# Layer 3 of five images: y not stored and loaded back, but convolved again from the residual in the closing loop

## The chip, the core and the metric

One core of one Trainium2 chip runs the whole program. The metric is the device time of one execution in microseconds (us). The kernel before takes 2627.5 us, the median of 3 runs (2625.96 to 2628.13).

The engines are named as in the profile: PE is TensorE (matrix products), DVE is VectorE, ACT is ScalarE, POOL is GpSimd, and SP is SyncE, which here only issues transfers (DMAs). Each engine works through its own queue in order.

## The reference, cut to what matters

The input `x` is 16 images of 64 channels by 128 by 128, fp32. Four layers follow each other, each a residual branch on a group-normalised input:

```python
x = x + _L0_conv_ref(_gn(x), L0_conv_conv_w)
x = x + _L1_conv_ref(_gn(x))
x = x + _L2_conv_ref(_gn(x), L2_conv_W, L2_conv_b)
x = x + _L3_conv_ref(_gn(x), L3_conv_w_bin, ...)
```

Layer 3 is the one that the change touches:

```python
y = _conv(x, w_bin, [(1, 1), (1, 1)])
y = _conv(y, w1x1, [(0, 0), (0, 0)]) + b1x1[None, :, None, None]
mean = jnp.mean(y, axis=(0, 2, 3), keepdims=True)
var = jnp.var(y, axis=(0, 2, 3), keepdims=True)
y = (y - mean) * jax.lax.rsqrt(var + EPS)
...
y = jnp.where(y >= 0, y, LEAK * y)
return jnp.clip(y, 0.0, CEIL)
```

Its mean and variance run over all 16 images. So no output of layer 3 can be finished before the last image has been convolved. Clipping at 0 makes the leaky branch vanish: the result is min(relu(y * scale + shift), 255), added to the residual.

## The kernel before

The image is cut by rows. A half image has 64 rows; a chunk is 8 rows of both halves, so an image has 8 chunks (`NS`), and a tile of one chunk has 128 partitions (64 channels, two halves) by 1024 elements, 512 KB. Three stages, `Front` (layers 0 and 1), `Layer2` and `Layer3`, run as a software pipeline: in each step, each stage does one chunk, of different images, in four quarters (`q` = 0 to 3). The order of the instructions on every engine is the order in which the Python code issues them (`InOrder`, line 63, keeps it); one helper on line 73 issues everything, which is why the profile puts nearly every instruction down to L73. The stages pass images through DRAM: `x2_d` after layer 1, `x3_d` after layer 2 (the residual that layer 3 adds to) and `y_d` after layer 3's convolution.

Layer 3's two convolutions are folded into one 3x3 convolution with 64x64 weights per tap (`w3`, line 209, filled by `weights_of_layer_3`). `Layer3.at` makes y of a chunk from differences and sums of rows, adds up its mean and its squares (`bn_sum`, `bn_sq`), and one step later stores it to `y_d` with four DMAs (from line 1040), each of 64 partitions with rows of 512 bytes.

After the last chunk the closing part begins. `parts` (line 1095) lists 128 pieces, 8 for each image; a piece is a tile of 128 partitions with 4 KB of an image in each (`whole`, line 1098: two partitions to a channel). For each piece, `fetch` (line 1113) takes two free tiles from `room` and loads y and the residual into them. `room` is filled, from 8 steps before the last image's first chunk of layer 3 was due, with the buffers that earlier stages no longer need, 38 tiles in all; one piece is fetched in every step from there on (line 1175), then as many as there is room for. From line 1187 the sums become a scale `sc` and a shift `sh`. Then the closing loop (line 1212) runs over all pieces: one ACT Relu over y, one DVE operation that takes the minimum with 255 and adds the residual, one store of 512 KB to `out`, and a new fetch when more than 8 tiles are free.

Products of two fp32 operands appear as two records each on PE. Products that use only 64 rows and 64 columns of the array can run four abreast, one in each quarter; `section` issues layer 2's and layer 3's remaining products in that way.

Of the kernel before, what the change touches and what calls it, by code (L numbers as in the profile page):

```python
# [10 lines left out]
F32 = mybir.dt.float32  # L11
AF = mybir.ActivationFunctionType
ALU = mybir.AluOpType
AX = mybir.AxisListType

B, C, H, W = 16, 64, 128, 128
P = 128
HW = H * W
HH = H // 2
NP = H // 2  # L20
R = 8
NS = HH // R
EARLY = 3
CP = 4
GN_EPS = 1e-5
BN_EPS = 1e-5
# [14 lines left out]
TO_PAIRS = [(0, 0, 0, 1), (0, 0, 1, 0), (0, 1, 0, 0), (1, 0, 1, 2), (1, 1, 0, 2), (1, 1, 1, 1)]  # L41
# [68 lines left out]
def tile_kernel(ctx: ExitStack, tc: tile.TileContext, x, cw_h, w2_t, b2, wbin_t, w1_t, b1, gamma, beta, consts, out):  # L110
    nc = tc.nc
    pe, dve, act, sp, pool = (InOrder(tc, e) for e in (nc.tensor, nc.vector, nc.scalar, nc.sync, nc.gpsimd))
    PSUM = bass.MemoryType.PSUM

    cpool = ctx.enter_context(tc.tile_pool(name="cpool", bufs=1))
# [5 lines left out]
    def k(name):  # L121
        return kc[:, AT[name][0]:AT[name][1]]

    def const(shape, name):
        return cpool.tile(shape, F32, name=name)

    cwh = const([P, C], "cwh")
    b2_sb, b1_sb, gamma_sb, beta_sb = (const([P, 1], n) for n in ("b2_sb", "b1_sb", "gamma_sb", "beta_sb"))
    bn_sum = cpool.tile([P, B * NS], F32, name="bn_sum")
    bn_sq = cpool.tile([P, B * NS], F32, name="bn_sq")  # L130

# [2 lines left out]
    x3_d = [dram.tile([C * HW], F32, name=f"x3_d{b}") for b in range(B)]  # L134
# [21 lines left out]
    ring = ctx.enter_context(tc.tile_pool(name="ring", bufs=2))  # L156
    stp = ctx.enter_context(tc.tile_pool(name="stp", bufs=2))
    ps_two = ctx.enter_context(tc.tile_pool(name="ps_two", bufs=2, space=PSUM))
    ps_one = ctx.enter_context(tc.tile_pool(name="ps_one", bufs=1, space=PSUM))
    ps_po = ctx.enter_context(tc.tile_pool(name="ps_po", bufs=1, space=PSUM))  # L160
# [289 lines left out]
    rows = []  # L450
# [363 lines left out]
    class Layer2:  # L814
# [55 lines left out]
        def done(self, co):  # L870

            edge = {}
            for half in ("lower", "upper"):
                edge[half] = sv(f"edge_{half}", 2)
                pool.tensor_scalar_mul(edge[half], co[:, 0:2], k(half))
            coefs3[self.b] = co, edge

        def square(self, i):
            act.activation(
# [99 lines left out]
    class Layer3:  # L979
# [34 lines left out]
        def at(self, i, q):  # L1014
            b = self.b
            n = b * NS + i
            if q == 0 and 0 <= i < NS:
                t = self.v[i]
                one = ps_one.tile([P, CP, W], F32, tag="one", name=f"one3_{b}_{i}")
                two = ps_two.tile([P, 2, CP, W], F32, tag="two", name=f"two3_{b}_{i}")  # L1020
                self.p[i] = two, one
                shared(one, w3[:, 2], t)
                if not both_layers(now[0]):
                    own(two[:, 0], 0, TO_PAIRS, w3, d3, packed["pk3"], d2[0])
            if q == 1:
                if 0 <= i < NS:
                    two, one = self.p[i]
                    if both_layers(now[0]):
                        for k in range(2):
                            own(two[:, k], k, TO_PAIRS, w3, d3, None)  # L1030
                        apart(two, TO_PAIRS, w3, d3)
                    else:
                        own(two[:, 1], 1, TO_PAIRS, w3, d3, packed["pk3"], d2[0])
                    self.v.pop(i)
                    self.c = ring.tile([P, CP * W], F32, tag="c3", name=f"c3_{b}_{i}", bufs=1)
                    act.activation(self.c, flat(one), AF.Identity, bias=b1_sb)
                if i + 1 < NS:
                    self.prepare(i + 1)
                if 1 <= i:
                    y = self.y.pop(i - 1)  # L1040
                    for s in range(2):
                        for z in range(2):
                            v = pairs(y_d[b], s)[:, (i - 1) * R:i * R, :].rearrange("c (n z) w -> c z n w", z=2)
                            sp.dma_start(v[:, z], y[s * C:(s + 1) * C, z])
            if q == 2:
                alone = not both_layers(now[0] + 1)
                if i + 1 < NS and alone:
                    even, odd, _ = self.v[i + 1]
                    difference(d3, spread(even, W), odd)
# [12 lines left out]
            if q == 3:  # L1062
                if i + 1 < NS and not both_layers(now[0] + 1):
                    self.twin()
                if 0 <= i < NS:
                    act.activation(
                        junk, self.y[i].rearrange("p s j w -> p (s j w)"), AF.Square,
                        accum_out=bn_sq[:, n:n + 1],
                    )
# [22 lines left out]


    N = R * W
    parts = [(b, q) for b in range(B) for q in range(C * HW // P // N)]
    room, loaded = deque(), deque()

    def whole(d, q):
        return d.rearrange("(p n) -> p n", p=P)[:, q * N:(q + 1) * N]

    def rest(pool, tag, shape, bufs, n=None):
        for m in range(bufs if n is None else n):
            t = pool.tile([P] + shape, F32, tag=tag, name=f"end_{tag}_{len(room)}", bufs=bufs)
            while len(t.shape) > 2:
                t = t.rearrange("p a b c -> p (a b) c" if len(t.shape) == 4 else "p a b -> p (a b)")
            room.append(t[:, 0:N])
# [5 lines left out]

    def fetch():
        n = fetched[0]
        if n < len(parts):
            b, q = parts[n]
            yt, rt = room.popleft(), room.popleft()
            sp.dma_start(yt, whole(y_d[b], q))
            sp.dma_start(rt, whole(x3_d[b], q))
            loaded.append((yt, rt))  # L1120
            fetched[0] += 1

    for step in range(starts[2][1] - 2, steps):
        now[0] = step
        for q in range(4):
# [46 lines left out]
                n = 3 if step == last_one else 1 if step < last_one + NS - 2 else 0  # L1172
                rest(ring, "x3", [2, CP, W], NS + 2, n)

            if step >= last_one - NS and q == 3 and len(room) > 1:
                fetch()
    while chains:
        tick()
    rest(ring, "x3", [2, CP, W], NS + 2, NS + 2 - 3 - (NS - 3))
    rest(ring, "y", [2, CP, W], 2)  # L1180
    rest(ring, "v3", [R + 2, W], 2)
    while len(room) > 1:
        fetch()

    mv = cpool.tile([P, 2], F32, name="mv")
    dve.tensor_reduce(mv[:, 0:1], bn_sum, axis=AX.X, op=ALU.add)
    dve.tensor_reduce(mv[:, 1:2], bn_sq, axis=AX.X, op=ALU.add)

    pm = sm(2)
    pe.matmul(pm, k("bnavg"), mv, start=True, stop=True)
    me = cpool.tile([P, 2], F32, name="me_bn")
    dve.tensor_copy(me, pm)
    var = cpool.tile([P, 1], F32, name="var_bn")
    dve.scalar_tensor_tensor(var, me[:, 0:1], me[:, 0:1], me[:, 1:2], op0=ALU.mult, op1=ALU.subtract)
    dve.tensor_scalar(var, var, -1.0, BN_EPS, op0=ALU.mult, op1=ALU.add)
    sd = cpool.tile([P, 1], F32, name="sd_bn")
    act.activation(sd, var, AF.Sqrt)
    r0 = cpool.tile([P, 1], F32, name="r0_bn")  # L1200
    dve.reciprocal(r0, sd)
    e = cpool.tile([P, 1], F32, name="e_bn")
    dve.scalar_tensor_tensor(e, var, r0, r0, op0=ALU.mult, op1=ALU.mult)
    dve.tensor_scalar(e, e, -0.5, 1.5, op0=ALU.mult, op1=ALU.add)
    sc = cpool.tile([P, 1], F32, name="sc")
    dve.tensor_mul(sc, r0, e)
    dve.tensor_mul(sc, sc, gamma_sb)
    sh = cpool.tile([P, 1], F32, name="sh")
    dve.tensor_mul(sh, me[:, 0:1], sc)
    dve.tensor_sub(sh, beta_sb, sh)  # L1210

    for b, q in parts:
        yt, rt = loaded.popleft()
        act.activation(yt, yt, AF.Relu, bias=sh, scale=sc)
        dve.scalar_tensor_tensor(rt, yt, 255.0, rt, op0=ALU.min, op1=ALU.add)
        sp.dma_start(whole(out[b].rearrange("c h w -> (c h w)"), q), rt)
        room.extend((yt, rt))

        if len(room) > 8:
            fetch()  # L1220


# [36 lines left out]
```

## Time and profile before

| what | value |
|---|---|
| median of 3 runs | 2627.5 us |
| the profiled execution, its own time | 2633.98 us |
| its span, first to last instruction | 2632.2 us |
| PE busy | 2068.1 us, 79% of the span, 15748 records |
| DVE busy | 2085.6 us, 79% |
| ACT busy | 1988.8 us, 76% |
| POOL busy | 410.9 us, 16% |
| DMA, read from and written to DRAM | 346.23 MB and 268.44 MB |
| granted PE clock, mean | 0.892 |

How to read it. The page gives busy time of each engine, then the span in 40 equal slices of 65.8 us: each digit is an engine's busy share of that slice in tenths (9 is 90% or more), and two rows below give the mean busy share of the core's 16 DMA engines and what they moved. A second part is the chain of waits: followed back from the last instruction, at each step to what released it. A third lists groups of equal instructions by engine, operation, output and input tile: count, busy time in us, mean of one in ns, then the idle time before them and what ended it. The table of stretches gives the same busy times for chosen windows, with the granted PE clock, the DMA share and GB/s. In SP's rows an `SPq` entry is the issue of a DMA; the transfer itself lands later. Tile names come from the program; `end_...` are the free tiles of the closing part, and `xw`, `xh`, `d2b` and `q` are older buffers used as such.

### The profile page before, as it was taken

Reading aid. Unit: us, or ns where it says so; the run is one execution under the profiler, and the core shown is the slowest. Engines: PE = TensorE matmul, PEld = TensorE weight load, DVE = VectorE, ACT = ScalarE, POOL = GpSimd, SP = SyncE. Lnnn points to the kernel's source line nnn. Section 1 sums busy time; section 2 is a strip of 40 time slices with the busy share of each in tenths; the row PEclk is TensorE's granted clock in tenths of the full one; section 3 lists DMA queues with packets and bytes.
Section 4 is the critical chain, followed back from the end, with each engine's and each line's share of the span. In section 5 each row is a group of like instructions: output and inputs, shape, how many; then the busy total and the mean of one; then the engine's idle time right before and its main releaser. Section 6 shows DMA issues by size and latency. Waiting matters only on the chain.

```text
span 2632.2 us, 45566 instructions
## 1 busy us (share of the span) xinstructions
PE 2068.1 (79%) x15748; PEld 822.4 (31%) x15748; DVE 2085.6 (79%) x2759; ACT 1988.8 (76%) x3297; POOL 410.9 (16%) x623
## 2 busy tenths in 40 slices
PE   6578899999999999999999999999999990000000
PEld 4333433434343434333333433333333330000000
DVE  4998989999999999999999999999994335333332
ACT  4778889898989898989989888888986575333332
POOL 3332322112111112121212122111101000000000
PEclk8689999999999999999999999999999995555555
DMA  8789979898888888888989877787867779999999
GB/s 206 203 230 240 238 187 240 210 235 217 231 227 222 224 221 228 216 225 219 245 210 250 201 192 202 191 209 201 211 173 184 201 211 372 419 419 419 419 419 376
DMA packets 682261, 654.48 MB, mean 249 GB/s; under 512 B 56320, under 2 KB 576672, under 8 KB 682032
## 3 DMA queue, kind: packets, MB, share of 16 engines
q1 hardware_dynamic: 668208, 613.83, 80.5%
q0 software_dynamic: 13824, 37.75, 5.5%
q8 instruction: 125, 2.05, 0.3%
q14 instruction: 104, 0.85, 0.1%
HBM read 346.23 MB, written 268.44 MB: 234 GB/s over the span
## 4 chain that ended last, share of the span: by engine, by line
PE 45%; DMA 23%; DVE 11%; ACT 9%; SPq 7%; issue 3%; POOL 0%; DVEq 0%; ACTq 0%; POOLq 0%
PE two L73 23%; PE one L73 15%; SPq L73 7%; DVE u L73 4%; PE bank L73 3%; PE po L73 3%; ACT v L73 2%; DVE e L73 2%; DMA v<-x_d 2%; DMA end_x<-x_d 2%; DMA out<-end_x 2%; DMA x_d<-u 2%; DMA x<-in_x 2%; DMA out<-xw 2%; DMA end_x<-y_d 2%
## 5 line engine op out<-in xcount | busy, mean ns | idle before, releaser
L73 PE MATMUL two<-d,w 64*64 64x512 f32 (+2 forms) x2992 | 692.4, 593 | 0.0
L73 PE MATMUL one<-v,w 128*64 128x508 f32 (+2 forms) x1600 | 362.5, 585 | 11.3 <-ACT c L73 10.8
L73 PE MATMUL one<-v,wi 128*64 128x508 f32 (+3 forms) x1536 | 350.9, 591 | 0.0
L73 PEld LDWEIGHTS two<-d,w 64*64 64x64 f32 (+1 forms) x2992 | 206.7, 134 | 415.1 <-issue 406.7
L73 DVE SCALAR_TENSOR_TENSOR e<-e 128x1032 f32<-128x1032 f32 (+1 forms) x256 | 313.3, 1224 | 0.0
L73 ACT ACTIVATE xh<-po,co 128x128 f32<-128x128 f32 (+1 forms) x480 | 274.4, 621 | 24.8 <-PE po L73 19.8
L73 DVE SCALAR_TENSOR_TENSOR y<-two,c 128x1024 f32<-128x1024 f32 x128 | 156.2, 1221 | 93.4 <-ACT v L73 63.4
L73 PE MATMUL po<-x,abd 64*64 64x512 f32 (+1 forms) x1024 | 189.5, 623 | 49.8 <-ACT xh L73 46.5
L73 PE MATMUL two<-q,cross 64*64 64x508 f32 (+3 forms) x944 | 216.1, 573 | 0.0
L73 ACT ACTIVATE v<-x,co 128x1024 f32<-128x1024 f32 (+3 forms) x256 | 203.8, 847 | 0.0
L73 ACT ACTIVATE v<-v,co 128x1154 f32<-128x1154 f32 x128 | 172.1, 1345 | 28.6 <-DMA v<-x_d 24.0
L73 DVE TENSOR_TENSOR d<-v 128x1024 f32<-128x1024 f32 x128 | 156.3, 1221 | 47.0 <-ACT v L73 29.2
L73 DVE SCALAR_TENSOR_TENSOR u<-xh 128x1170 f32<-128x1170 f32 x128 | 175.9, 1374 | 12.1 <-DMA x_d<-u 5.9
L73 POOL DMA_DIRECT2D q<-d2b x138 | 72.1, 526 | 721.5 <-DVE d2b L73 412.9
L73 PE MATMUL two<-d2a,wi 128*64 128x508 f32 (+1 forms) x768 | 183.2, 589 | 0.0
L73 PE MATMUL two<-d2b,wi 128*64 128x508 f32 (+3 forms) x768 | 176.6, 569 | 0.0
L73 PEld LDWEIGHTS one<-v,w 128*64 128x64 f32 x1600 | 110.3, 137 | 209.7 <-issue 162.7
L73 DVE SCALAR_TENSOR_TENSOR u<-xh,co,u 128x1024 f32<-128x1024 f32 x128 | 163.9, 1280 | 15.0 <-ACT u L73 14.9
L73 POOL DMA_DIRECT2D q<-d2a x138 | 73.8, 537 | 642.1 <-issue 276.1
L73 DVE SCALAR_TENSOR_TENSOR u<-e,co,u 128x1024 f32<-128x1024 f32 x128 | 164.2, 1283 | 8.2 <-DVE u L73 0.5
L73 DVE SCALAR_TENSOR_TENSOR x<-two,c 128x1024 f32<-128x1024 f32 x128 | 156.7, 1225 | 14.5 <-ACT junk L73 0.5
L73 ACT ACTIVATE edges<-v,co 64x8 f32<-64x8 f32 x512 | 156.3, 305 | 11.0 <-POOL co L73 0.9
(174 smaller groups left out, 3687.1 us busy)
## 6 DMA issues: line engine op xcount, KB each, us to landing
x<-in_x SPq DMA_DIRECT2D x256, 256.0 KB, 4.1
x_d<-u SPq DMA_DIRECT2D x512, 128.0 KB, 3.2
y_d<-y SPq DMA_DIRECT2D x512, 128.0 KB, 3.5
x_d<-x SPq DMA_DIRECT2D x496, 128.0 KB, 2.8
xr<-in_x SPq DMA_DIRECT2D x120, 512.0 KB, 5.8
v<-x_d SPq DMA_DIRECT2D x448, 72.1 KB, 3.0
v<-x_d SPq DMA_DIRECT2D x224, 144.2 KB, 2.9
end_x<-x_d SPq DMA_DIRECT2D x39, 512.0 KB, 10.0
```

Source lines behind the costliest of these rows:

```text
L73: return self.tc.keep_in_program_order(call(*args, **kwargs))
```

## The change

`AGAIN` names images 3 to 7. For them:

- `Layer3.at` still makes y and adds its mean and squares to the sums, but y isn't stored. The layer's norm coefficients of these images are kept (`kept`).
- In the closing part they have 40 chunks in place of 40 pieces. A list `todo` mixes the 40 chunks with the 88 pieces of the other images: two chunks, eight pieces, then chunks with one or two pieces between, and eight pieces after the last. For a chunk, `fetch` takes one tile and loads the residual alone, in the half-image layout: two DMAs of 64 partitions by 4 KB.
- A chunk goes through stages in three turns of the loop. `again_in` normalises its residual into a `v3` tile with one row above. `again_close` adds the row below, which comes from the next chunk, and `again_products` issues 36 products of 64x64 by 512 (nine taps, two groups of four rows, two halves), and two products with the identity that bring the second four rows' residual to the other half. `again_out` does a Relu and a min-and-add for each group of four rows, and stores 512 KB in four DMAs of 64 partitions by 2 KB.
- The sums are turned into two scales and shifts, one for each layout. `v3`'s two tiles leave `room`, so it has 36. In each step before the closing loop, fetching goes on until at least two tiles have been asked for.
- Ten DMAs of 32 KB bring the rows next to the middle of the five images into `w2`, which is free by then.

The diff, without the constants' layout and the small arithmetic of the scales:

```diff
+AGAIN = (3, 4, 5, 6, 7)
...
             coefs3[self.b] = co, edge
+            if self.b in AGAIN:
+                pool.tensor_copy(kept[:, AGAIN.index(self.b)], co[:, 0:2])
...
                     y = self.y.pop(i - 1)
-                    for s in range(2):
+                    for s in range(0 if b in AGAIN else 2):
...
-    parts = [(b, q) for b in range(B) for q in range(C * HW // P // N)]
-    room, loaded = deque(), deque()
+    parts = deque((b, q) for b in range(B) if b not in AGAIN for q in range(C * HW // P // N))
+    again = deque((b, i) for b in AGAIN for i in range(NS))
+    todo, ahead, behind = [], 8, 6
+    share = len(parts) - ahead - behind
+    for n in range(NS * len(AGAIN)):
+        todo.append(("again",) + again.popleft())
+        while n > 0 and len(todo) - n - 1 < ahead + (n - 1) * share // (NS * len(AGAIN) - 2):
+            todo.append(("loaded",) + parts.popleft())
+    todo += [("loaded",) + part for part in parts]
...
     def fetch():
...
+        else:
+            t = room.popleft()
+            for h in range(2):
+                sp.dma_start(t[cols(h)], halves(x3_d[b], h, q * R, R))
+            loaded.append((t,))
+        fetched[0] += 1
+        return len(loaded[-1])
+
+    def again_in(b, i, t):
...
+        v = ring.tile([P, R + 2, W], F32, tag="v3", name=f"v_again_{b}_{i}")
+        r = t.rearrange("p (j w) -> p j w", w=W)
+        if i == 0:
+            pool.memset(v[lo, 0, :], 0.0)
+            again_norm(n, v[hi, 0, :], xe[hi, n], hi)
+        else:
+            again_norm(n, v[:, 0, :], at_hand[-1][1][:, R - 1, :])
+        again_norm(n, v[:, 1:R + 1, :], r)
+        at_hand.append((v, r, b, i))
...
+            if step == last_one + NS - 1 and q == 2:
+                again_in(*todo[0][1:], loaded[0][0])
+
+            if step >= last_one - NS and q == 3:
+                n = 0
+                while n < 2 and len(room) > 1:
+                    n += fetch()
...
-    rest(ring, "v3", [R + 2, W], 2)
...
+    def again_products():
+
+        v, r, b, i = at_hand[-1]
+        two = ps_two.tile([P, 2, CP, W], F32, tag="two", name=f"two_again_{b}_{i}")
+        pool_, tag = ((ps_po, "po"), (ps_one, "one"))[(b * NS + i) % 2]
+        rest_ = pool_.tile([P, CP, W], F32, tag=tag, name=f"rest_again_{b}_{i}")
+        for h in range(2):
+            pe.matmul(rest_[cols(1 - h)], k("I")[cols(h), cols(h)], r[cols(h), CP:R, :], start=True, stop=True)
+        order = [(ky, kx) for kx in (1, 0, 2) for ky in range(3)]
+        for n, (ky, kx) in enumerate(order):
+            o0, o1 = (0, W) if kx == 1 else (1, W) if kx == 0 else (0, W - 1)
+            for g in range(2):
+                for h in range(2):
+                    j = g * CP + ky
+                    pe.matmul(
+                        two[cols(h if g == 0 else 1 - h), g, :, o0:o1], rows_of[ky, h][:, kx],
+                        v[cols(h), j:j + CP, o0 + kx - 1:o1 + kx - 1], start=n == 0, stop=n + 1 == len(order),
+                    )
+        summed.append((two, rest_, r, b, i))
+
+    def again_out():
+
+        two, rest_, r, b, i = summed.popleft()
+        to = out[b].rearrange("c h w -> (c h w)")
+        for g, (tag, add) in enumerate((("c2", r[:, 0:CP, :]), ("c3", rest_))):
+            z = ring.tile([P, CP * W], F32, tag=tag, name=f"z_{b}_{i}_{g}", bufs=1)
+            act.activation(z, flat(two[:, g]), AF.Relu, bias=shb, scale=sc[:, 1:2])
+            to_rows = flat(r[:, g * CP:(g + 1) * CP, :])
+            dve.scalar_tensor_tensor(to_rows, z, 255.0, flat(add), op0=ALU.min, op1=ALU.add)
+            for h in range(2):
+                sp.dma_start(halves(to, h if g == 0 else 1 - h, i * R + g * CP, CP), to_rows[cols(h)])
+        room.append(flat(r))
...
-    for b, q in parts:
-        yt, rt = loaded.popleft()
-        act.activation(yt, yt, AF.Relu, bias=sh, scale=sc)
-        dve.scalar_tensor_tensor(rt, yt, 255.0, rt, op0=ALU.min, op1=ALU.add)
-        sp.dma_start(whole(out[b].rearrange("c h w -> (c h w)"), q), rt)
-        room.extend((yt, rt))
-
-        if len(room) > 8:
+    for n, (way, b, q) in enumerate(todo):
+        if way == "again":
+            (t,) = loaded.popleft()
+            if n > 0:
+                again_close(t)
+                again_products()
+                coming.append((b, q, t))
+        else:
+            yt, rt = loaded.popleft()
+            act.activation(yt, yt, AF.Relu, bias=sh[:, 0:1], scale=sc[:, 0:1])
+            dve.scalar_tensor_tensor(rt, yt, 255.0, rt, op0=ALU.min, op1=ALU.add)
+            sp.dma_start(whole(out[b].rearrange("c h w -> (c h w)"), q), rt)
+            room.extend((yt, rt))
+            if len(summed) > 1 or summed and n > len(todo) - 3:
+                again_out()
+            if coming:
+                again_in(*coming.popleft())
+            elif n == len(todo) - behind + 1:
+                again_close(None)
+                again_products()
+        while len(room) > 8 and fetched[0] < len(todo):
             fetch()
+    while summed:
+        again_out()
```

More of the change, by code (lines that the diff above doesn't have):

```diff
@@ L127, in tile_kernel @@
     cwh = const([P, C], "cwh")
-    b2_sb, b1_sb, gamma_sb, beta_sb = (const([P, 1], n) for n in ("b2_sb", "b1_sb", "gamma_sb", "beta_sb"))
+    b2_sb, b1_sb = (const([P, 1], n) for n in ("b2_sb", "b1_sb"))
+    gamma_sb, beta_sb = (const([P, 2], n) for n in ("gamma_sb", "beta_sb"))
+    kept = const([P, len(AGAIN), 2], "kept")
     bn_sum = cpool.tile([P, B * NS], F32, name="bn_sum")
@@ L1094, in tile_kernel, with again_norm @@
     N = R * W
-    parts = [(b, q) for b in range(B) for q in range(C * HW // P // N)]
-    room, loaded = deque(), deque()
+    parts = deque((b, q) for b in range(B) if b not in AGAIN for q in range(C * HW // P // N))
[7 more added lines that the diff above has]
+    todo += [("loaded",) + part for part in parts]
+    room, loaded, at_hand = deque(), deque(), deque(maxlen=2)
+    def again_norm(n, dst, src, rows=slice(0, P)):
+        act.activation(dst, src, AF.Identity, bias=kept[rows, n, 1:2], scale=kept[rows, n, 0:1])
     def whole(d, q):
@@ L1114, in fetch @@
         n = fetched[0]
-        if n < len(parts):
-            b, q = parts[n]
+        if n == len(todo):
+            return 2
+        way, b, q = todo[n]
+        if way == "loaded":
             yt, rt = room.popleft(), room.popleft()
@@ L1120, in fetch @@
             loaded.append((yt, rt))
-            fetched[0] += 1
+        else:
[6 more added lines that the diff above has]
+    def again_in(b, i, t):
+        n = AGAIN.index(b)
+        v = ring.tile([P, R + 2, W], F32, tag="v3", name=f"v_again_{b}_{i}")
[7 more added lines that the diff above has]
+        at_hand.append((v, r, b, i))
     for step in range(starts[2][1] - 2, steps):
@@ L1173, in tile_kernel @@
                 rest(ring, "x3", [2, CP, W], NS + 2, n)
-            if step >= last_one - NS and q == 3 and len(room) > 1:
-                fetch()
+            if step == starts[1][1] + NS * B + 1 and q == 0:
+                xe = w2.rearrange("p a k c -> p (a k c)")[:, 0:len(AGAIN) * W].rearrange("p (b w) -> p b w", w=W)
+                for n, again_b in enumerate(AGAIN):
+                    for h, row in ((0, HH), (1, HH - 1)):
+                        sp.dma_start(
+                            xe[cols(h), n], x3_d[again_b].rearrange("(c r w) -> c r w", c=C, w=W)[:, row, :]
+                        )
[5 more added lines that the diff above has]
+                    n += fetch()
     while chains:
@@ L1180, in tile_kernel @@
     rest(ring, "y", [2, CP, W], 2)
-    rest(ring, "v3", [R + 2, W], 2)
-    while len(room) > 1:
+    while len(room) > 1 and fetched[0] < len(todo):
         fetch()
@@ L1189, in tile_kernel @@
     dve.tensor_reduce(mv[:, 1:2], bn_sq, axis=AX.X, op=ALU.add)
[L1191 to L1198, printed above, removed]
+    pm = sm(4)
@@ new lines, in tile_kernel, with pair @@
+    pe.matmul(pm[:, 0:2], k("bnavg"), mv, start=True, stop=True)
+    pe.matmul(pm[:, 2:4], k("same"), mv, start=True, stop=True)
+    me = cpool.tile([P, 2, 2], F32, name="me_bn")
+    dve.tensor_copy(me[:, 0], pm[:, 0:2])
+    dve.tensor_scalar_mul(me[:, 1], pm[:, 2:4], 1.0 / (B * HW))
+    mean, square = me[:, :, 0], me[:, :, 1]
+    def pair(name):
+        return cpool.tile([P, 2], F32, name=name)
+    var = pair("var_bn")
+    dve.tensor_mul(var, mean, mean)
+    dve.tensor_sub(var, square, var)
@@ L1199, in tile_kernel @@
+    dve.tensor_scalar_add(var, var, BN_EPS)
+    sd = pair("sd_bn")
     act.activation(sd, var, AF.Sqrt)
-    r0 = cpool.tile([P, 1], F32, name="r0_bn")
+    r0 = pair("r0_bn")
     dve.reciprocal(r0, sd)
-    e = cpool.tile([P, 1], F32, name="e_bn")
-    dve.scalar_tensor_tensor(e, var, r0, r0, op0=ALU.mult, op1=ALU.mult)
+    e = pair("e_bn")
+    dve.tensor_mul(e, var, r0)
+    dve.tensor_mul(e, e, r0)
     dve.tensor_scalar(e, e, -0.5, 1.5, op0=ALU.mult, op1=ALU.add)
-    sc = cpool.tile([P, 1], F32, name="sc")
+    sc = pair("sc")
@@ L1206, in tile_kernel @@
     dve.tensor_mul(sc, r0, e)
     dve.tensor_mul(sc, sc, gamma_sb)
-    sh = cpool.tile([P, 1], F32, name="sh")
-    dve.tensor_mul(sh, me[:, 0:1], sc)
+    sh = pair("sh")
+    dve.tensor_mul(sh, mean, sc)
     dve.tensor_sub(sh, beta_sb, sh)
-    for b, q in parts:
-        yt, rt = loaded.popleft()
-        act.activation(yt, yt, AF.Relu, bias=sh, scale=sc)
-        dve.scalar_tensor_tensor(rt, yt, 255.0, rt, op0=ALU.min, op1=ALU.add)
-        sp.dma_start(whole(out[b].rearrange("c h w -> (c h w)"), q), rt)
-        room.extend((yt, rt))
-        if len(room) > 8:
+    shb = cpool.tile([P, 1], F32, name="shb")
@@ new lines, in tile_kernel, with again_close @@
+    dve.scalar_tensor_tensor(shb, sc[:, 1:2], b1_sb, sh[:, 1:2], op0=ALU.mult, op1=ALU.add)
+    rows_of = {(kk, i): w3[cols(i), slot, :, cols(o)] for slot, i, o, kk in TO_PAIRS}
+    def again_close(r_next):
+        v, _, b, i = at_hand[-1]
+        n = AGAIN.index(b)
+        if i + 1 == NS:
+            pool.memset(v[hi, R + 1, :], 0.0)
+            again_norm(n, v[lo, R + 1, :], xe[lo, n], lo)
+        else:
+            again_norm(n, v[:, R + 1, :], r_next[:, 0:W])
+    def again_products():
[14 more added lines that the diff above has]
+                        v[cols(h), j:j + CP, o0 + kx - 1:o1 + kx - 1], start=n == 0, stop=n + 1 == len(order),
+                    )
+        summed.append((two, rest_, r, b, i))
@@ new lines, in tile_kernel @@
+    rows_of = {(kk, i): w3[cols(i), slot, :, cols(o)] for slot, i, o, kk in TO_PAIRS}
+    summed, coming = deque(), deque()
+    for n, (way, b, q) in enumerate(todo):
[5 more added lines that the diff above has]
+                coming.append((b, q, t))
+        else:
+            yt, rt = loaded.popleft()
[11 more added lines that the diff above has]
+        while len(room) > 8 and fetched[0] < len(todo):
@@ L1244 @@
         "b1": both(L3_conv_b1x1),
-        "gamma": twice(L3_conv_gamma),
-        "beta": twice(L3_conv_beta),
+        "gamma": laid(np.concatenate([twice(L3_conv_gamma), both(L3_conv_gamma)], axis=1)),
+        "beta": laid(np.concatenate([twice(L3_conv_beta), both(L3_conv_beta)], axis=1)),
         "consts": constants(),
```

## The prediction

> **What bounds the kernel now.** I read the 40 slices of the page first, because the kernel has a long first part and a short last one.
>
> ```profile
> PE   6578899999999999999999999999999990000000
> ...
> DMA  8789979898888888888989877787867779999999
> GB/s 206 203 230 240 238 187 240 210 235 217 231 227 222 224 221 228 216 225 219 245 210 250 201 192 202 191 209 201 211 173 184 201 211 372 419 419 419 419 419 376
> ```
>
> For 33 slices of 65.8 us TensorE (PE) is full; in the last seven it does nothing and the transfers run flat at 419 GB/s. So there are two bounds, one after the other: PE to about 2185 us, DMA from there to 2632.2 us. The chain of waits says the same from 2184 us on, and nothing else stands in it:
>
> ```profile
> 2184.56 3.51 DVE xw L73 x3
> 2188.08 9.34 DMA out<-xw
> 2197.48 10.29 DMA out<-end_xr
> 2207.79 10.00 DMA xh<-x_d
> 2217.86 9.95 DMA end_xr<-y_d
> ```
>
> The tail's groups and the DMA queue's own waits, both taken from 2200 to 2600 us, show who waits for whom there:
>
> ```profile
> L73 ACT ACTIVATE end_x<-end_x,sh,sc 128x1024 f32<-128x1024 f32 x34 | 41.9, 1238 | 79.5 <-DMA end_x<-y_d 79.5
> ...
> SPq L73 <- DMA out<-end_x: 30.1, 34, 0.9
> ```
>
> ScalarE (ACT) waits for loads to land, and SyncE (SP) waits for earlier transfers to land before it issues the next; a transfer takes 10.0 us from issue to landing and one ends every 1.25 us, so eight are always out. Compute in the tail is hidden as long as it keeps up on average, since loads run 15 pieces ahead of the stores. What counts in the tail is therefore the sum of DMA time.
>
> That time isn't bytes alone. The table of stretches (core-wide: length, busy time of each engine, granted clock, DMA share, GB/s) has two places where the only traffic of weight is loads of 64 partitions by 4 KB, alternating between the lower and the upper half (x_first at 9 to 14 us, x at 46 to 49 us):
>
> ```profile
> core 0: us, PE busy (x) PEld busy (x) DVE busy (x) ACT busy (x) POOL busy (x), PEclk, DMA share, GB/s
> 9.00:14.00 5.00, 3.62 (x24) 2.92 (x24) 1.10 (x2) 0.61 (x1) 4.64 (x9) 1.00 1.04 237
> 46.00:49.00 3.00, 0.00 (x0) 0.00 (x1) 2.96 (x3) 3.00 (x5) 0.00 (x0) 1.00 1.00 243
> 2300.00:2600.00 300.00, 0.00 (x0) 0.00 (x0) 96.81 (x79) 97.44 (x80) 0.00 (x0) 0.50 1.03 419
> ```
>
> Share 1.0 in all three, but 240 GB/s for 64 partitions against 419 for the tail's 128-partition tiles. This is the line the forecast hangs on.
>
> [...]
>
> **The change, part by part.**
>
> *Tail, transfers removed and added.* Price of a 128-partition tile of 512 KB: 524,288 B / 419 GB/s = 1.251 us. Before, 128 pieces move three such tiles each: 384. After, 88 pieces make 264, and 40 chunks each load 512 KB in two 64-partition DMAs and store 512 KB in four of 64 partitions by 2 KB. At the time the closing loop begins, all tiles of the room have been asked for: 38 before; 36 after (the two v3 tiles no longer belong to it), which by the order of `todo` are chunks 0 to 5 and 15 pieces, so 6 chunk loads and 30 whole tiles. Left for the tail: 346 whole tiles before; 234 whole tiles, 34 chunk loads and 40 chunk stores after. With P for 512 KB of chunk traffic, the tail changes by 74 P - 112 x 1.251 = 74 P - 140.1 us. It breaks even at P = 1.89 us, that is 277 GB/s.
>
> For loads the nearest row is the 240 GB/s above, the same shape (64 partitions, 4 KB each, halves alternating): P = 2.18 us. For stores no row shows 64 partitions by 2 KB. [...] I take 2.18 us for stores too[...]. Sum: 74 x 2.18 - 140.1 = **+21.5 us**.
>
> Could mixing heal it? A chunk's transfers stand between 128-partition ones in the same queue[...]. The x_first loads didn't show it: 237 GB/s with eight out. I keep it for the range.
>
> *PE.* A chunk has 36 products of 64x64 by 512 columns, four side by side, and two identity products: ten rounds. The price is in the timeline, where layer 2 and layer 3 products stand four abreast (each fp32 product makes two records):
>
> ```profile
> 2043.65 0.59 PE L73 MATMUL two<-d,w 64*64 64x512 f32 x2
> 2043.67 0.59 PE L73 MATMUL two<-q,pk 64*64 64x512 f32 x2
> 2044.08 0.59 PE L73 MATMUL two<-d,w 64*64 64x512 f32 x2
> 2044.10 0.59 PE L73 MATMUL two<-q,cross 64*64 64x512 f32 x2
> 2044.51 0.59 PE L73 MATMUL two<-d,w 64*64 64x512 f32 x2
> ```
>
> From 2043.65 to 2044.51 is one round of four: 0.86 us. A chunk is 8.6 us, 40 are 344 us. A turn (one chunk and 74/38 = 1.95 pieces between) costs DMA 2 x 2.18 + 1.95 x 3.75 = 11.7 us. PE at 8.6 lies inside it, with 3.1 us to spare, so it costs nothing; if the cover were gone (chunk traffic at full rate: 2.50 + 7.31 = 9.8 us a turn) it would still fit by 1.2 us.
>
> *ACT, VectorE (DVE), SP in a turn.* ACT: one 128x1024 norm 1.24 us, two rows at most 0.49 each, two 512-column Relus at 0.68 (the row c<-one), 1.95 Relus at 1.24: 6.0 us. DVE: 1.95 x 1.22 and two half-size passes, about 3.6 us. SP: 12 issues of 0.33 to 0.65 us (`out` and `y_d` rows), 4 to 7.7 us. All under 11.7; hidden by the DMA sum. The Relu of a chunk stands on ACT ahead of later pieces and waits for PE, and its stores on SP ahead of later loads; but it is issued a whole turn after its products began, 11.7 us against 8.6, so nobody waits.
>
> *First part.* 160 stores of y go (20.97 MB) out of SP's queue, about 0.65 us of issue each. In the five stretches of images 3 to 7 (711 to 1335 us) PE is busy 615.6 of 624 us, so the most to be had is 8.4 us; the waits list puts PE's idle time there on ACT and DVE, not on a DMA. I take -2 us (0 to -8).
>
> *Handing over.* The first chunk's norm, 1.24 + 0.33 us on ACT, stands before the last Square, where ACT has room:
>
> ```profile
> 2179.05 1.06 ACT L73 ACTIVATE junk<-y 128x1024 bf16<-128x1024 f32 x1 [2.88 <-DVE y L73]
> ```
>
> so it costs nothing (1.6 us if that gap weren't there). The statistics get one more product and some five small DVE operations of 0.16 us, and the first row of chunk 0 to close before the first piece: +1 us (0 to 1.5, as transfers already issued go on meanwhile). Ten small loads of 32 KB pass through SP before the last y stores: 0 (up to 3). The five small Pool copies and the memsets are off every path: 0.
>
> **Sum.** 21.5 - 2 + 1 = +20.5 us. The profiled execution has a span of 2632.2 us within 2633.98; it becomes about 2652.7. Its time is 0.25% above the median shown, 2627.5, so I add the difference to the median: **2648 us**.
>
> **Rivals.**
> 1. *Chunk traffic at full rate, both ways* (ends faster). Place: the 64-partition loads and stores of the tail. Price: 74 x 1.251 - 140.1 = -47.5 us, with the other terms 2627.5 - 48.5 = 2579 us. It decides once chunk traffic averages over 277 GB/s. For it: [...] the sum of bytes falls by 10%. Against: 237 and 243 GB/s measured for just this shape.
> 2. *Only loads are slow; stores run at full rate.* 34 x 2.18 + 40 x 1.251 - 140.1 = -16 us, so 2611 us. [...] Against: nothing shown; it is merely unmeasured.
> 3. *PE becomes the bound.* If the half clock held all through [...], a chunk would take 17.2 us: 2184 + 40 x 17.2 + 15 for the last pieces = 2887 us. [...]
>
> **Chances.** Forecast (chunk traffic at 210 to 270 GB/s): 0.60, its own range 2632 to 2668. Rival 1: 0.17. Rival 2: 0.14. Rival 3: 0.03. Between break-even and the forecast [...]: 0.06, about 2628. The range to hold the time 8 times in 10 takes in rival 2 and not rival 1: 2608 to 2672. About 0.2% (5 us) is what a measurement here can tell from no change. Faster: 0.17 + 0.14 + 0.03 = 0.34; same: 0.05; slower: 0.61.
>
> **What would show it.** Right: in the tail a DMA share of about 1.0 at some 360 GB/s instead of 419, the 64-partition transfers slower per byte than whole tiles, PE idle about a quarter of each turn, ACT still ended by loads. Wrong: GB/s near 419 all along with an earlier end (rival 1); PE busy above 9 tenths and waits of ACT on `two_again` (rival 3); a first part that ends more than 8 us earlier.

## The result, and the profile after

| | median of its runs | lowest to highest | ratio to before, 95% interval |
|---|---|---|---|
| before | 2628.49 us (22 runs) | 2622.65 to 2646.89 | |
| after | 2638.92 us (22 runs) | 2628.18 to 2648.05 | 1.0032, 1.0018 to 1.0046 |

The change made the kernel 0.32% slower, 8.4 us by the ratio, where +20.5 was forecast. The direction was right, the size less than half. Below, microseconds worked out from ratios are the ratio times 2628. Differences between two kernels are taken from their ratios, since before's median on one chip and another lay between 2626.5 and 2628.8. The profiled execution of after took 2648.05 us (span 2645.9), 0.35% above its own median; its rates are read, not its end.

The 40 slices of after, rows of TensorE, DMA share and GB/s:

```profile
PE   6578899999999999999999999999999999978783
...
DMA  8799879898977777686878878787867679999999
GB/s 206 205 228 229 235 188 239 213 239 220 232 195 182 197 186 207 171 225 166 213 202 235 206 190 203 194 210 194 214 173 189 187 218 356 362 375 346 338 350 351
```

In the last seven slices, where PE was idle before, it is now 70 to 90% busy until the last; the DMA share is still full, but 419 GB/s have become 338 to 375. The table of stretches shows the same for after's closing loop (length, then busy us and count of PE, PEld, DVE, ACT, POOL; PE clock, DMA share, GB/s):

```profile
2200.00:2300.00 100.00, 99.98 (x888) 39.26 (x882) 41.34 (x44) 63.12 (x79) 0.40 (x2) 1.00 1.01 360
2300.00:2460.00 160.00, 131.26 (x1072) 50.97 (x1076) 50.12 (x56) 79.65 (x98) 0.80 (x4) 0.98 1.01 360
```

There are two regimes: at first PE has no gap, later it is busy 82%. The rate is 360 GB/s in both. The groups from 2200 to 2600 us (busy us, mean ns, idle before and what ended it) say who waits:

```profile
L74 PE MATMUL two_again<-v_again,w 64*64 64x508 f32 (+1 forms) x2664 | 335.4, 608 | 30.9 <-ACT v_again L74 30.9
...
L74 ACT ACTIVATE z<-two_again,shb,sc 128x512 f32<-128x512 f32 x72 | 51.6, 765 | 24.2 <-PE two_again L74 24.2
L74 ACT ACTIVATE end_x<-end_x,sh,sc 128x1024 f32<-128x1024 f32 x25 | 30.9, 1236 | 39.4 <-DMA end_x<-y_d 39.3
```

ACT waits for PE (the Relu of a chunk, `z`) as well as for loads, and PE for ACT. From these lines alone, transfers and TensorE are both suspects. That is what the experiments had to separate.

Ahead of the loop no loss is seen. ACT's timeline at the handing over, after (start us, length us; in brackets idle time before and what ended it):

```profile
2172.47 0.49 ACT L74 ACTIVATE v_again<-w,kept 64x128 f32<-64x128 f32 x1
2172.97 1.24 ACT L74 ACTIVATE v_again<-xw,kept 128x1024 f32<-128x1024 f32 x1
2175.31 1.06 ACT L74 ACTIVATE junk<-y 128x1024 bf16<-128x1024 f32 x1 [1.10 <-DVE y L74]
```

The first chunk's norm stands before the last Square, and the Square still has to wait 1.10 us for DVE: the norm was hidden. The last Square begins 3.7 us earlier than before (2175.31 against 2179.05). From one trace each this can't be told from chance: in later runs with the same first part as after it begins at 2169.93 (E9), 2170.81 (E3), 2174.16 (E2) and 2174.78 us (E12).

### The profile page after: what moved, and what is told of

Same layout as the page of the kernel before. It is cut to its first block, busy times and chain, and to the rows that moved or that the text cites. A ratio compares the mean times of both kernels' runs of the same rounds, so it can differ in the third digit from the quotient of the medians.

```text
span 2645.9 us, 52043 instructions
## 1 busy us (share of the span) xinstructions
PE 2435.8 (92%) x18790; PEld 961.9 (36%) x18790; DVE 2086.8 (79%) x2803; ACT 2070.9 (78%) x3457; POOL 413.5 (16%) x638
## 4 chain that ended last, share of the span: by engine, by line
PE 43%; DMA 19%; DVE 15%; ACT 9%; SPq 8%; issue 4%; POOL 1%; DVEq 0%; ACTq 0%; POOLq 0%
PE two L74 21%; PE one L74 14%; SPq L74 8%; DVE u L74 5%; PE bank L74 3%; DVE e L74 3%; PE two_again L74 3%; ACT v L74 3%; DMA out<-end_x 2%; PE po L74 2%; DMA x_d<-u 2%; DVE d L74 2%; DMA v<-x_d 2%; DVE y L74 2%; DMA out<-end_y 1%
## 5 line engine op out<-in xcount | busy, mean ns | idle before, releaser
L74 PE MATMUL two_again<-v_again,w 64*64 64x508 f32 (+1 forms) x2880 | 365.1, 613 | 39.1 <-ACT v_again L74 39.1
L74 PEld LDWEIGHTS two_again<-v_again,w 64*64 64x64 f32 x2880 | 134.8, 137 | 242.6 <-issue 177.2
L74 PEld LDWEIGHTS one<-v,wi 128*64 128x64 f32 x1536 | 101.0, 137 | 192.7 <-issue 154.9
```

The source lines that it names most:

```text
L74: return self.tc.keep_in_program_order(call(*args, **kwargs))
```

## The experiments

**E1 to E3: a chunk's load whole, its store whole, one tap.** The theories are named in the texts of the expectations. The edits, each alone, on the changed kernel:

```diff
 E1
-            for h in range(2):
-                sp.dma_start(t[cols(h)], halves(x3_d[b], h, q * R, R))
+            sp.dma_start(t, whole(x3_d[b], q))
 E2
-            for h in range(2):
-                sp.dma_start(halves(to, h if g == 0 else 1 - h, i * R + g * CP, CP), to_rows[cols(h)])
...
+        sp.dma_start(whole(to, i), flat(r))
 E3
-        order = [(ky, kx) for kx in (1, 0, 2) for ky in range(3)]
+        order = [(1, 1)]
```

> The changed kernel, but a chunk's residual comes as one DMA of 128 partitions by 4 KB in the pieces' layout instead of two of 64 partitions; the channels then stand in another order, so the convolved values of the five images aren't the reference's. Time of the changed kernel: 2638.9 us. Theory A (the 64-partition loads are the dear part, about 2.9 us for 512 KB; stores cost near full rate): 34 x (2.9 - 1.25) = 56 us less, about 2583. Theory B (loads cost 2.18 us as in the forecast, the stores are as dear): 34 x 0.93 = 32 us less, about 2607. Theory C (the closing loop is held by the waits of ACT and PE, not by transfers): less than 10 us less, above 2629.

> The changed kernel, but a chunk is stored by one DMA of 128 partitions by 4 KB in the pieces' layout instead of four of 64 partitions by 2 KB; rows of the five images land in another order. Theory A (stores run near full rate, about 1.4 us for 512 KB): 40 x 0.15 = 6 us less, and up to 6 more from an end that no longer runs through small stores: 2627 to 2633. Theory B (the forecast's 2.18 us): 40 x 0.93 = 37 us less, about 2602. Theory C: no difference, 2635 to 2643.

> The changed kernel with one of the nine taps of the repeated convolution, so 4 of 36 products; the five images' layer 3 is left incomplete. Theory A (transfers bound the closing loop): 2633 to 2643, no difference; at most 5 us less, from the first 100 us where PE was full. Theory C (PE bounds it): PE's 344 us shrink to about 70, so 20 us less or more, below 2619.

| | median | ratio to before, 95% interval | against after |
|---|---|---|---|
| E1 load whole | 2608.1 us | 0.9922, 0.9910 to 0.9934 | -28.9 us |
| E2 store whole | 2627.26 us | 1.0003, 0.9988 to 1.0017 | -7.6 us |
| E3 one tap | 2641.18 us | 1.0062, 1.0044 to 1.0081 | +7.9 us |

The same stretch, 2200 to 2460 us, of E3. The bytes are those of after:

```profile
2200.00:2460.00 260.00, 88.85 (x300) 25.16 (x300) 87.76 (x97) 138.57 (x170) 1.19 (x6) 0.58 1.02 361
```

PE is busy a third of the time and the rate stays at 361 GB/s, and nothing was gained. So TensorE doesn't bind the changed kernel. E3 is even 7.9 us (2 to 14) slower than after; why isn't shown. The idle times of ACT before `z` were real, but they weren't what set the end. Making the load whole gave about what the forecast's price implies (0.93 us each on 34 loads is 32 us); making the store whole gave 0.19 us each, not 0.93. I concluded then that stores of 64 partitions are cheap. That conclusion fell later.

**E4: the first part alone.** The kernel before, with y of images 3 to 7 not stored; the closing loop loads y of images 8 to 12 in its place.

```diff
-                    for s in range(2):
+                    for s in range(0 if 3 <= b < 8 else 2):
...
-            sp.dma_start(yt, whole(y_d[b], q))
+            sp.dma_start(yt, whole(y_d[b + 5 if 3 <= b < 8 else b], q))
```

> The kernel before, without the stores of y for images 3 to 7; the closing loop reads another image's y in their place, so the output of the five images isn't the reference's. Transfers of the closing loop stay as they were. It shows what the first part gains when these 160 stores go. Forecast: 2 us less. By the two profiles (the sums of the statistics begin at 2179.0 before and 2175.3 after): 4 us less, about 2624.5. Rival: nothing, 2628.

Measured: 2626.61 us, ratio 0.9992 (0.9979 to 1.0005). Leaving out the 160 stores changed nothing that can be told from noise (-5.5 to +1.3 us); -2 us is in the interval, and so is 0. That fits stores hidden behind TensorE.

**E5, E6: both whole; the same with one tap.** The edits of E1 and E2 together (E5), and the same with all taps but one left out (E6).

> Both the chunk's load and its store as one 128-partition transfer of 512 KB each; everything else as in the changed kernel. The computation is changed: a chunk's load brings 128 partitions of one image's neighbouring rows in place of the same 64 channels of two row halves, and its store writes whole tiles, so the output is another's; bytes and instruction counts of the engines stay. Theory T (the transfers' shape is all that the tail loses): 74 tiles at the whole pieces' 1.251 us less 140.1 us saved = -47.5, so about 2580. Theory S (a second loss of about 15 us that doesn't come from the shape: the TensorE-bound start of the closing loop, the drain at the end): the gains of the two single runs add up, 30.8 + 11.7 = 42.5 off 2638.9, so about 2596. If the two single runs counted the same gain twice: 2605 or more.

> As the run with both transfers whole, with one of the nine taps of the second convolution of a chunk left out but one (1 of 9 computed). Theory TensorE: the closing loop's start, where chunks lie prefetched and TensorE runs without a gap, costs the 15 us: this run is at 2580 while its sibling with nine taps is at 2596. Theory drain/DMA: no difference between the two, within 3 us.

Measured: E5 2585.04 us, ratio 0.9837 (0.9813 to 0.9860); E6 2582.87 us, ratio 0.9828 (0.9805 to 0.9851). Their stretches, E5 and then E6:

```profile
2200.00:2460.00 260.00, 252.89 (x2216) 101.22 (x2210) 103.48 (x112) 159.49 (x197) 1.59 (x8) 1.00 1.03 416
```

```profile
2200.00:2460.00 260.00, 101.01 (x348) 28.36 (x340) 102.21 (x112) 159.60 (x197) 1.59 (x8) 0.62 1.03 418
```

With whole transfers the loop runs at 416 GB/s, as before the change, though PE is busy 97% of it. The shape of the chunks' transfers (their partitions, the length of their rows and the number of DMAs together) is the whole loss: 51.2 us (44 to 58) between after and E5. Theory T (2580) is nearer than S (2596), and E6 isn't faster than E5 beyond the intervals, so TensorE at the loop's start wasn't the missing 15 us. But the single gains, 28.9 + 7.6 = 36.5 us, don't add up to 51.2. This left a question: where one kind alone is made whole, less is gained.

**E9 to E13: transfers taken away.** From the changed kernel: the 40 stores of chunks are taken away, or most of the loads of chunks, or both; E11 to E13 are also without eight of nine taps.

```diff
 E9, E11, E12
-            for h in range(2):
-                sp.dma_start(halves(to, h if g == 0 else 1 - h, i * R + g * CP, CP), to_rows[cols(h)])
 E10, E11, E13
-            for h in range(2):
-                sp.dma_start(t[cols(h)], halves(x3_d[b], h, q * R, R))
+            if not again_seen(t):
+                for h in range(2):
+                    sp.dma_start(t[cols(h)], halves(x3_d[b], h, q * R, R))
 E11, E12, E13
-        order = [(ky, kx) for kx in (1, 0, 2) for ky in range(3)]
+        order = [(ky, kx) for kx in (1, 0, 2) for ky in range(3)][:1]
```

(`again_seen` is true for a buffer of the program that a load has gone to before; slices of one buffer, such as those of `xw`, count as one.)

The expectations speak of 7 loads that stay and 33 that go. The traces of E10, E11 and E13 show ten chunk loads of 256 KB, so 5 chunks are loaded and 35 aren't. In after, six chunk loads are issued before the first Relu of the closing loop (2180.15 us), and the seventh follows at 2189.2 us. So 34 loads of the closing loop are missing, as many as the prediction counted, and the prices below are worked out with 34 loads and 40 stores.

> The changed kernel without the 40 stores (512 KB each, as four 64-partition transfers) of its chunks; their part of the output is not written. What the time falls by, over 40, is a store's price. By the forecast (2.18 us each): 2638.9 - 87 = 2552. By what the two whole-store runs gave (11.7 us of shape over 40 with split loads, 20.9 with whole loads, on 1.25): 1.54 to 1.77 each, so 2568 to 2577.

> The changed kernel with only the first 7 of 40 chunk loads: the other 33 chunks are computed from what the buffer held, so their part of the output is another's. What the time falls by, over 33, is a load's price. By the forecast (2.18 us each): 2638.9 - 72 = 2567. By the whole-load runs (30.8 us of shape over 33 with split stores, 43.5 with whole stores, on 1.25): 2.18 to 2.57 each, so 2554 to 2567. TensorE can't be done before about 2535.

> Neither those 33 loads nor the 40 stores, and one tap of nine, so that only the whole pieces move in the closing loop: what they cost alone. At 1.251 us a tile: 2627.5 - 140 = 2487. If the whole pieces were slower for another reason than the chunks' traffic beside them (the order, the 8 in flight, the end), this run is above 2487 by that much: 2495 to 2503.

> No chunk stores (their output is not written) and one tap of nine: whole pieces and the split chunk loads only, TensorE out of the way. Against the run with neither (ratio 0.9471, 2489 us), the rise over 33 is a load's price. Forecast's price 2.18: 2489 + 72 = 2561. A dear load of 2.57 (from the whole-load run beside whole stores): 2574. If TensorE was no part of the matter, the time stays at the 2587 of the run with nine taps (2.98 each).

> Only the first 7 chunk loads (the other chunks are computed from what the buffer held, so their output is another's) and one tap of nine: whole pieces and the split chunk stores only. The rise over the run with neither, by 40, is a store's price. Forecast's price 2.18: 2489 + 87 = 2576, as with nine taps. A cheap store of 1.54: 2550; of 1.25 (full rate): 2539. If load and store come out together at 147 us, nothing arises from their mixture; if at much less, the mixture costs the rest.

| what chunks transfer | median | ratio, 95% interval | above E11 | per 512 KB |
|---|---|---|---|---|
| E11 nothing, one tap | 2488.18 us | 0.9471, 0.9457 to 0.9485 | | |
| E12 split loads (34), one tap | 2573.99 us | 0.9784, 0.9751 to 0.9818 | 82 us | 2.4 us |
| E13 split stores (40), one tap | 2573.98 us | 0.9787, 0.9766 to 0.9807 | 83 us | 2.1 us |
| E3: both, split, one tap | 2641.18 us | 1.0062, 1.0044 to 1.0081 | 155 us | 2.10 us |
| after: both, split, nine taps | 2638.92 us | 1.0032, 1.0018 to 1.0046 | 147 us | 1.99 us |
| E5: both, whole, nine taps | 2585.04 us | 0.9837, 0.9813 to 0.9860 | 96 us | 1.30 us |
| E9 split loads, nine taps | 2587.4 us | 0.9855, 0.9838 to 0.9871 | 101 us | |
| E10 split stores, nine taps | 2575.4 us | 0.9802, 0.9787 to 0.9816 | 87 us | |

E11 first: with the chunks' traffic gone, the whole pieces cost what the 419 GB/s of before says, and no more. Its ratio is 139.0 us (135 to 143) below before; 112 tiles by 1.251 us are 140.1. Order, start and end of the new loop lose nothing beyond this interval.

E12 and E13 then price each kind alone: a split load 2.4 us (2.1 to 2.7), a split store 2.1 us (1.9 to 2.2), each beside whole pieces. So stores of 64 partitions by 2 KB are *not* cheap, and E2's reading of them was wrong.

The packets of the traces show where each price is paid. A packet is one record of a DMA engine in the trace: 4 KB, one partition's part, of a whole tile or a split load, and 2 KB of a split store (in after, 2300 to 2600 us: 22510 of 4096 bytes and 6649 of 2048). In E11 a packet of 4 KB takes 160 ns on average (2200 to 2440 us; the next figures are from 2200 to 2460 us), and 2% of them take over 165 ns. In E12 their mean is 181 ns, and 25% take over 165 ns. In E13 the stores' own packets, those of 2 KB, take 85 ns on average, which is 385 GB/s over 16 DMA engines. There the mean of the 4-KB packets, all of whole tiles, rises to 173 ns: about 1.4 us of a store's price is time of its own packets (256 of 85 ns over 16 engines), and about 0.65 us is lost by the tiles beside it. So what a split store costs beyond a whole one is lost mostly by others. Why isn't shown.

Do the two kinds cost less together than one by one? Alone they cost 82 + 83 = 165 us. The run with both and one tap, E3, costs 155 us: 10 us less, with an interval of -2 to 22, which holds 0. After, with nine taps, costs 147 us: 18 us less (6 to 29), but it differs from E12 and E13 in the taps too. The whole-transfer runs, all with nine taps, give 51.2 - 36.5 = 15 us (6 to 23). They have a rival: TensorE could have held back E2, as it held back E9 (below). E2 is 57.6 us (48 to 67) above E12; 40 whole stores at 1.251 us are 50.0 of that, which leaves 7.5 us (-2 to 17) for the taps. E2 with one tap, which would settle it, wasn't run. So an overlap of loads and stores is likely but not shown, and no run shows what would cause it.

The stretches of E10 and E13 hold a warning about busy shares. They differ only in eight taps:

```profile
2200.00:2460.00 260.00, 260.00 (x2314) 105.41 (x2310) 111.51 (x119) 166.07 (x209) 1.59 (x8) 1.00 1.01 376
```

```profile
2200.00:2460.00 260.00, 103.01 (x360) 28.90 (x360) 107.50 (x119) 166.92 (x209) 1.59 (x8) 0.61 1.01 380
```

In E10 PE is busy 260 us of 260, and ACT's `z` waits for it, from 2200 to 2460 us:

```profile
L74 ACT ACTIVATE z<-two_again,shb,sc 128x512 f32<-128x512 f32 x60 | 43.3, 771 | 69.4 <-PE two_again L74 69.4
```

Yet E13, with PE at 40%, ends at the same time (0.9802 and 0.9787, 4 us apart, -3 to 11). In E9, with 247 of 260 us busy, taking the taps away did help, by 19 us (9 to 28), so what E9 by itself gave for a store (46.5 / 40 = 1.16 us) was too low. Neither a full row nor a wait on an engine says that it sets the end; the run without its work does. A look at the end of the row helps too: in E10 PE's last product ends at 2539.7 us, 33 us before the span's end (2572.3).

**E7, E8: chunks that reach all partitions.** Two images share a chunk: 64 channels of each, the same 8 rows. The residuals of two images lie next to each other in DRAM, so a chunk's load is one DMA of 128 partitions. The second four rows still leave in two 64-partition stores, since their products end in the other half. E7 takes 4 images, E8 takes 6.

```diff
-AGAIN = (3, 4, 5, 6, 7)
+AGAIN = (4, 5, 6, 7)
...
-            for h in range(2):
-                sp.dma_start(t[cols(h)], halves(x3_d[b], h, q * R, R))
+            sp.dma_start(t, x3_pair[b].rearrange("(p r) -> p r", p=P)[:, q * N:(q + 1) * N])
...
-            for h in range(2):
-                sp.dma_start(halves(to, h if g == 0 else 1 - h, i * R + g * CP, CP), to_rows[cols(h)])
+            if g == 0:
+                sp.dma_start(to[:, at], to_rows)
+            else:
+                for h in range(2):
+                    sp.dma_start(to[cols(1 - h), at], to_rows[cols(h)])
```

> Four images' y not stored (4 to 7) instead of five; a chunk holds 64 channels of two neighbouring images, so that its load is one 128-partition DMA of 4 KB a partition, no copy of the residual's other half is wanted; the stores of the first channel half one 128-partition DMA of 2 KB, of the second two 64-partition ones. All is computed as in the kernel before. By transfers alone: 30 tiles fewer at 1.251 us = -37.5, stores' shape about +5: 2596. With the 15 us that the changed kernel also loses: about 2609. If the 64-KB pitch between partitions and not their number made the loads slow (E1's load had another pitch), the gain of E1 is absent here and the time is about 2630 or more.

> The same with six images (2 to 7). By transfers alone: 46 tiles fewer at 1.251 us = -57.6, stores' shape +7: 2578. TensorE: 48 chunks x 8.55 us = 410 us from 2177 on, ending about 2590 to 2600: with TensorE as the bound 2597 to 2609.

Measured: E7 2590.92 us, ratio 0.9862 (0.9839 to 0.9884); E8 2594.8 us, ratio 0.9876 (0.9855 to 0.9897). Both beat both kernels; E7 is 36 us faster than before, by 30 tiles fewer at 1.251 us (37.5). Its slices:

```profile
PE   6568899999999999999999999999999999977773
...
DMA  8789979888888777777778887777877768999999
GB/s 207 203 238 245 239 189 242 215 235 225 230 225 224 194 195 194 182 199 187 205 192 239 211 199 192 200 201 200 214 188 178 203 199 271 413 416 415 397 417 387
```

With 397 to 417 GB/s in the loop, the loss is gone. E7's load has the same distance between partitions (one channel, 64 KB) and the same 4 KB as the split load; so the stride wasn't what cost. What is left is the number of partitions or the number of DMAs, since E7 also puts one DMA of 512 KB in the place of two of 256 KB; no run splits a 128-partition load in two. The traces speak for the partitions: in the stretch that the forecast rests on, the packets themselves are slow. From 9 to 14 us in the trace of before, a 4-KB packet takes 284 ns on average, against 159 ns in the tail. The remaining split stores, a quarter of the chunks' traffic, cost too little to be seen here.

E8 moves less and isn't faster. From its chain of waits, near the end:

```profile
2552.28 7.75 PE two_again L74 x70
2560.04 0.36 PE rest_again L74 x2
...
2560.83 7.75 PE two_again L74 x70
...
2577.91 7.71 PE two_again L74 x66
```

Chunks follow each other in 8.55 us without a gap, and PE is busy all 350 us from 2200 to 2550; the rate there, 393 GB/s, is below what E5 reached. By transfers alone 2578 was expected. Here the row is full up to the end: PE's last product ends at 2585.6 us, 8 us before the span's end (2593.5), and from 2550 to 2586 us PE is busy 35.6 of 36 us. So faster transfers alone could have ended E8 only some 8 us sooner. This makes TensorE its bound, unlike E10's; the run with fewer taps wasn't made.

## Why the prediction was right or wrong

- *Bound after the change: DMA time.* Right. E3 and E6 show it: with one tap in place of nine, nothing was gained.
- *Whole tiles: 112 fewer at 1.251 us, -140.1.* Right: E11 gives -139.0 with the first part and the handing over in it; the three terms together were forecast at -141.1.
- *Chunk traffic: 74 x 2.18 us.* This term failed, and it is the whole miss. Forecast were 161.7 us (21.5 + 140.1); measured are 147 us (142 to 153), 1.99 us each (1.92 to 2.06). That is 14 us less; the other terms give 2 us back, and 20.5 - 8.4 = 12.1 us remain. In it:
  - *Loads at 240 GB/s, 2.18 us.* Not contradicted, perhaps low: alone 2.4 us (2.1 to 2.7).
  - *Stores taken at the loads' price.* Right in size for stores alone, 2.1 us (1.9 to 2.2), but by luck: it was the author's estimate, carried over from the loads, since no row of before showed such stores. It took the stores' own rate to be 240 GB/s, and in E13 their own packets ran at 385 GB/s; the rest was lost by the tiles beside them.
  - *"Could mixing heal it? ... The x_first loads didn't show it."* Here the step went wrong. The prices were multiplied out as if each transfer had the DMA to itself. The row used as evidence was loads with loads, and the case to be priced was loads with stores beside a busy TensorE. The single prices add up to 165 us, more than the forecast's; after pays 18 us less than that. With equal taps the difference is 10 us (-2 to 22), and the run with nine taps is 8 us (2 to 14) faster than the one with one. So how much of the 18 us is an overlap of loads and stores, and how much a matter of TensorE's pace, stays open.
- *Rival 2, only loads slow (2611 us)*: wrong, by E13. For a while E2 seemed to support it.
- *Rival 1, full rate (2579 us)*: wrong for the change, but it is what E5 comes near with whole transfers, 2585.
- *PE, 8.6 us a chunk, hidden.* The price was right: 8.55 in E8. Rival 3's 17.2 us a chunk didn't appear: the granted clock was 1.00 and 0.98 in after's two stretches. "Idle about a quarter of each turn" holds roughly later in the loop (18% idle), not in its first 100 us, where chunks lie prefetched.
- *The signs.* The sign of being right, some 360 GB/s, came: 360. A sign of rival 3 came too, ACT waiting for `two_again` (24.2 us), and E3 shows that it didn't set the end.
- *The chances.* Rival 3 ends later (2887 us), so its 0.03 doesn't belong in the sum of "faster", if that is what the 0.03 there stands for.
- *First part -2, handing over +1.* Not contradicted: E4 gives 0.9992 for the first part, whose interval holds -2 and 0; the norm on ACT was hidden as said.

## What to carry to other kernels

When a change recomputes data to save traffic, look at the shape of the traffic that stays. Here 10% fewer bytes in the tail made the kernel slower, because the chunks' transfers were split by halves of the partitions (51.2 us between after and E5); with loads laid out over all 128, with four images in place of five, the same idea won 1.4%. Prices taken one kind at a time needn't add up for a mixture; bound the mixture from both sides, by the sum and by the dearer kind alone (165 and 83 us here, for 147 in after and 155 in E3).

Undoing a cost while its partner stays can hide it: E2 alone told a false story that E13 corrected. Take each kind away with everything else out of the way before naming the cheap one, and set the results against a run with both kinds that has everything else out of the way too: E3, not after.

## What the runs showed of the hardware that had not been expected

- Split transfers of 64 partitions cost 2.4 us (loads) and 2.1 us (stores) per 512 KB alone, 1.99 us on average together in after and 2.10 us in E3; whole ones cost 1.30 us in E5. A store's own packets aren't slow (85 ns for 2 KB in E13).
- A few split loads slow more than themselves. In E12's window from 2300 to 2460 us:

```profile
2300.00:2460.00 160.00, 58.01 (x192) 13.73 (x192) 57.18 (x63) 88.88 (x109) 0.80 (x4) 0.57 1.01 353
```

  Of the 108 tiles that are issued in this window, 16 are split loads. At 240 GB/s for these and 419 for the rest the mean would be 1 / (0.148 / 240 + 0.852 / 419) = 377 GB/s; it was 353. Split loads have 15% of the tiles, and 28% of the window's 4-KB packets take over 165 ns. The DMA share reads 1.01 here, about what it does at 419 (1.03): it counts a slow packet as busy, so the GB/s and not the share tell the loss.
- PE without one gap over 260 us (E10) cost nothing that can be told from noise (4 us, -3 to 11, against E13).
